# Layer 0's first graph convolution by seven block products, and the first LSTM weights loaded and summed at other places

## The chip, the cores and the metric

The kernel runs on one core of a Trainium2 chip. The metric is the device time of one launch in microseconds (us). Engines: TensorE (PE, with weight loads as PEld), VectorE (DVE), ScalarE (ACT), GpSimd (POOL) and SyncE (SP), which here only issues DMA transfers. All data are float32.

## What is computed

Four layers of a graph network over x, 128 graphs of 64 nodes with 256 features (8192 rows), each added to its input after a layer norm and a ReLU. The change is in layer 0:

```
h = relu(layernorm(x))
h = relu(adj @ (h @ Wg0 + bg0))
h = relu(adj @ (h @ Wg1 + bg1))
for p in 1..4:                      # windows of p nodes
    last = LSTM_p(windows of h)     # Wih[p-1], Whh[p-1], bih + bhh
    h at the last node of each window = last
x = x + h
```

Layers 1 to 3 (edge attention, two products with batch norms, dense attention) follow and stay as they are.

## The kernel before

The stage in question (L453 to L575) makes both graph convolutions for 16 chunks of 512 rows (CHUNK; two graphs fill 128 partitions, so a chunk is four tiles of 128 x 256). For each chunk a generator, graph_convolutions (L502), has five parts, with a yield between them:

1. Norm(...).all() (L78): on VectorE bn_stats and bn_aggr for each of four tiles (L87, L88), a root on ScalarE (L95), reciprocal and shift on VectorE (L96, L97), four scaled ReLUs on ScalarE into h (L109); then x of a later chunk is requested (load_x, L466).
2. aggregate (L139): eight products of 128 columns on TensorE with bdA, the block-diagonal adjacency, and two copies on VectorE into aggT (L145), whose halves k are features and whose columns are the chunk's nodes.
3. The first convolution: for each of two output halves c, two products of 512 columns with quarters of wg0 add up in a bank; VectorE adds bg0 times the row sums of adj (rsum) into h1T (L516), ScalarE takes the ReLU (L524). All products go through the helper mm, so L50 is the line of every one of them, and their tiles tell them apart: aggT,wg is this one.
4. The second convolution: eight products of 256 columns (wg,h1T), VectorE adds bg1 (L539), the result reuses aggT.
5. The second aggregation: eight products of 128 columns (bdA,aggT), ReLUs on ScalarE into hT or hop (L555); chunks 8 to 15 go to memory (hm).

The main loop over n starts chunk n and advances each chunk under way by one part: the newest first, then from the oldest on. So in turn n TensorE makes the second aggregation of chunk n - 4, the second convolution of n - 3, the first of n - 2 and the aggregation of n - 1. From n = 3 on, each step also advances a generator of tables for layers 1 and 2 (edge_tables, late_tables): mostly VectorE operations of 128 x 512, among them four DMA fills of a scatter field (L319), 2.3 MB each, on SP.

The order of an engine's queue is fixed before the launch by the framework's planner: from the program order as priority, it issues what it estimates to be ready first. An instruction passed to late() may not go ahead of what stands before it on its engine in program order. [...]

After turn 2 three sets of LSTM weights are made (Weights, L424): each is one 1 MB transfer on SP (L429) and four sums or differences of quarters on GpSimd, 128 x 512 each (L440). They are the operands of the LSTM's own products, which already use seven products of quarters (L651), with copies on ScalarE (L694, L699) and sums on VectorE (L695, L705, L710). The LSTM starts after the stage. A similar helper, quarter_sums (L126), makes layer 2's operands (L136). Eight PSUM banks are shared by the whole stage; a bank is free again when its last reader is done.

## Time and profile before

| what | value |
|---|---|
| time, median of 3 runs | 2069.58 us (2069.1 to 2072.04) |
| profiled execution: its own time | 2061.03 us |
| profiled execution: span of the core | 2059.3 us |
| TensorE busy in the span | 2006.1 us |
| first product of the LSTM starts at | 192.77 us |
| GpSimd busy in the span | 308.2 us |
| first convolution, 128 products' records of 128 x 512 | 58.5 us as recorded |

Recorded lengths of products overlap, so the pace of TensorE is read from start to start. A product of float32 shows as two records. In the rows, "out<-in" names tiles; behind it stand the shapes, the count, and busy time with the mean in ns, or in a timeline the start and length in us and in brackets the idle time before with what ended it. In the table of busy times each engine has the busy us of the stretch and a count of instructions.

### The profile page before, as it was taken

To read this page: it belongs to the slowest core of one execution; us is meant where nothing else is said; L and a number is where in the kernel's file an instruction comes from. 1 tells how busy PE (TensorE), PEld (TensorE's weight loads), DVE (VectorE), ACT (ScalarE), POOL (GpSimd) and SP (SyncE) were. 2 spreads that over 40 slices of the span, in tenths; PEclk is the share of its full clock that TensorE was granted. 3 is DMA by queue.
4 is the path that set the end of the run, shared out by engine and by line. 5 is a ranking of instruction groups with operands and counts; after the bars stand their busy time and mean duration, and the time that the engine had idled before them with its cause. 6 is when DMAs were issued, how large, how long until landed. Compare 5 with 4: busy or idle time off the path is not lost. (4 is left out here: it accounts for less than half of the span.)

```text
span 2059.3 us, 25491 instructions
## 1 busy us (share of the span) xinstructions
PE 2006.1 (97%) x9444; PEld 1346.1 (65%) x9444; DVE 1359.5 (66%) x2507; ACT 1184.4 (58%) x2230; POOL 308.2 (15%) x416
## 2 busy tenths in 40 slices
PE   8999999999999999999999999999999999999998
PEld 6777478866688845887667887333334775444786
DVE  8755666564565477566556555677777877886776
ACT  4344766555565457566446564666675556591544
POOL 3000010020110020002001000323223420000563
PEclk9999999999999999999999999999999999999999
DMA  9331000100100170001001003412223841022012
GB/s 316 98 98 51 0 21 1 42 0 1 41 1 1 40 246 21 1 0 42 0 1 41 1 16 120 138 61 97 72 98 122 298 154 52 0 82 82 32 62 72
DMA packets 63196, 135.06 MB, mean 66 GB/s; under 512 B 6240, under 2 KB 40928, under 8 KB 60768
## 3 DMA queue, kind: packets, MB, share of 16 engines
q1 hardware_dynamic: 56832, 109.11, 15.6%
q0 software_dynamic: 5632, 24.12, 3.1%
q8 instruction: 74, 1.21, 0.2%
q14 instruction: 50, 0.41, 0.1%
q10 hardware_dynamic: 608, 0.20, 0.0%
HBM read 87.28 MB, written 46.14 MB: 65 GB/s over the span
## 5 line engine op out<-in xcount | busy, mean ns | idle before, releaser
L651 PE MATMUL pa<-xop,sih 128*128 128x256 f32 (+2 forms) x1056 | 344.4, 418 | 11.7 <-DVE gate L705 8.2
L679 ACT ACTIVATE gate<-gate,bias 128x256 f32<-128x256 f32 (+2 forms) x368 | 247.4, 679 | 173.6 <-DVE gate L695 91.0
L651 PEld LDWEIGHTS pa<-xop,sih 128*128 128x128 f32 x1056 | 198.4, 190 | 87.9 <-issue 22.8
L651 PE MATMUL pc<-xop,wih 128*128 128x256 f32 (+2 forms) x736 | 251.2, 423 | 0.0
L695 DVE TENSOR_TENSOR gate<-pb,gate 128x256 f32<-128x256 f32 (+2 forms) x184 | 87.5, 475 | 225.7 <-PE pb L651 154.1
L651 PE MATMUL pa<-lstm_h,shh 128*128 128x256 f32 (+1 forms) x672 | 212.7, 398 | 0.0
L993 DVE SCALAR_TENSOR_TENSOR lr<-lr 128x1024 f32<-128x1024 f32 x128 | 151.1, 1222 | 55.3 <-ACT lr L992 55.3
L651 PEld LDWEIGHTS pc<-xop,wih 128*128 128x128 f32 x736 | 139.8, 190 | 51.2 <-issue 23.0
L710 DVE TENSOR_TENSOR gate<-pc,gate 128x256 f32<-128x256 f32 (+2 forms) x184 | 87.6, 476 | 121.2 <-PE pc L651 120.9
L992 ACT COPY lr<-pair 128x1024 f32<-128x1024 f32 x128 | 123.1, 1014 | 47.6 <-PE pair L986 47.6
L651 PEld LDWEIGHTS pa<-lstm_h,shh 128*128 128x128 f32 x672 | 127.7, 190 | 30.2
L651 PE MATMUL pc<-lstm_h,whh 128*128 128x256 f32 (+1 forms) x448 | 141.8, 398 | 0.0
L694 ACT COPY gate<-pa 128x256 f32<-128x256 f32 (+2 forms) x184 | 76.1, 413 | 96.7 <-PE pa L651 96.1
L986 PE MATMUL pair<-sd_hot,xq 64*128 64x512 f32 x512 | 127.5, 616 | 0.3 <-ACT lr L992 0.3
L705 DVE TENSOR_TENSOR gate<-pa,gate 128x256 f32<-128x256 f32 (+2 forms) x184 | 87.5, 475 | 44.0 <-PE pa L651 43.4
L970 PE MATMUL bank<-wlv,hT 128*128 128x512 f32 x240 | 110.7, 604 | 0.0
L699 ACT COPY gate<-pa 128x256 f32<-128x256 f32 (+2 forms) x184 | 75.4, 410 | 59.1 <-PE pa L651 57.9
L679 ACT ACTIVATE gate<-pa,bias 128x256 f32<-128x256 f32 (+2 forms) x184 | 94.0, 511 | 23.6 <-PE pa L651 22.0
L440 POOL TENSOR_TENSOR sih<-wih 128x512 f32<-128x512 f32 x8 | 10.7, 1335 | 630.6 <-DMA wih<-in_WihT 484.4
L651 PE MATMUL pa<-xop,wih 128*128 128x256 f32 (+1 forms) x320 | 101.4, 398 | 2.7 <-ACT xop L632 2.7
L651 PE MATMUL pb<-xop,wih 128*128 128x256 f32 (+1 forms) x320 | 100.3, 398 | 0.4 <-DVE gate L695 0.4
L651 PEld LDWEIGHTS pc<-lstm_h,whh 128*128 128x128 f32 x448 | 85.1, 190 | 20.1
(346 smaller groups left out, 3809.2 us busy)
## 6 DMA issues: line engine op xcount, KB each, us to landing
field<-sd_hot SPq DMA_DIRECT2D x4, 2304.0 KB, 17.2
wih<-in_WihT SPq DMA_DIRECT2D x8, 1024.0 KB, 5.1
xres<-in_x SPq DMA_DIRECT2D x16, 512.0 KB, 4.6
xa<-xres POOLq DMA_DIRECT2D x16, 512.0 KB, 5.2
dense<-field POOLq DMA_DIRECT2D x4, 2048.0 KB, 8.5
xin<-xb SPq DMA_DIRECT2D x16, 512.0 KB, 3.4
h<-xb SPq DMA_DIRECT2D x16, 512.0 KB, 3.2
xin<-in_x SPq DMA_DIRECT2D x15, 512.0 KB, 3.9
```

Source lines behind the costliest of these rows:

```text
L440: nc.gpsimd.tensor_tensor(o, x, y, op)
L651: ins = nc.tensor.matmul(p[:, : self.N], weights[kind, self.phase](k, q), x[k], start=first_ and kind == "ih", stop=kind == "hh" or not se ...
L679: nc.scalar.activation(out, in_, AF.Tanh if q == 2 else AF.Sigmoid, bias=bias[:, self.w - 1, 2 * q + j : 2 * q + j + 1],)
L694: nc.scalar.copy(blk[0, 0], pa[:, :N])
L695: nc.vector.tensor_tensor(blk[0, 0], pb[:, :N], blk[0, 0], ALU.add)
L699: nc.scalar.copy(blk[1, 0], pa[:, :N])
L705: nc.vector.tensor_tensor(blk[1, 1], pa[:, :N], blk[1, 1], ALU.add)
L710: nc.vector.tensor_tensor(blk[1, 0], pc[:, :N], blk[1, 0], ALU.add)
L970: ins = nc.tensor.matmul(p, hTs[n][:, k, i * P : (i + 1) * P], wlv[:, k, :], start=k == 0, stop=k == 1)
L986: ins = nc.tensor.matmul(p[:, par, :], queries[it][r, c * P : (c + 1) * P], sd_hot[r, :], start=True, stop=True)
L992: nc.scalar.copy(lr, p)
L993: nc.vector.scalar_tensor_tensor(lr, lr, 0.2, lr, ALU.mult, ALU.max)
```

## The change

The first convolution's 256 x 256 matrix is cut into four 128 x 128 quarters, and a chunk's aggT into four blocks of 128 features x 256 nodes. Seven products of one (sum of) quarters with one (sum of) blocks take the place of the eight quarter products (four of 512 columns). The sums of quarters are made once. Per chunk GpSimd forms four differences of blocks (side), and adds the bias rb (rsum times bg0) to three of the four output blocks; ScalarE copies three products out of PSUM, VectorE adds the rest in four sums of 256 columns, the last with the fourth bias. Three products accumulate in bank pa on what stands there, one in pc.

The generator now has twelve parts (four for the norm, one for the aggregation and the differences, four for the products, one for the second convolution, two for the second aggregation), and a written order says which chunk's next part comes when within a turn. x is requested with the aggregation, a turn later. The tables advance at five places of a turn. The three sets of LSTM weights are requested after turns 5, 7 and 9; their sums are issued two per turn from turn 6 on, each behind late().

```diff
--- before.py
+++ after.py
@@ -422,7 +422,7 @@
 
 
         class Weights:
-            def __init__(self, kind, w):
+            def __init__(self, kind, w, at_once=True):
                 bufs = 2 if kind == "ih" else 1
                 t = wsp.tile([P, 2, 4, 2, P], F32, tag=f"w{kind}", name=f"w{kind}", bufs=bufs)
                 s = wsp.tile([P, 3, 4, P], F32, tag=f"s{kind}", name=f"s{kind}", bufs=bufs)
@@ -431,14 +431,22 @@
                 )
                 a11, a12, a21, a22 = t[:, 0, :, 0, :], t[:, 1, :, 0, :], t[:, 0, :, 1, :], t[:, 1, :, 1, :]
                 s1, s2, s4 = s[:, 0], s[:, 1], s[:, 2]
-                for o, x, y, op in (
+                self.sums = [
                     (s1, a21, a22, ALU.add),
                     (s2, s1, a11, ALU.subtract),
                     (s4, a12, s2, ALU.subtract),
                     (a21, a11, a21, ALU.subtract),
-                ):
-                    nc.gpsimd.tensor_tensor(o, x, y, op)
+                ]
+                self.at_once = at_once
+                while at_once and self.sums:
+                    self.sum()
                 self.of = {1: a11, 2: a12, 3: s4, 4: a22, 5: s1, 6: s2, 7: a21}
+
+            def sum(self):
+                o, x, y, op = self.sums.pop(0)
+                ins = nc.gpsimd.tensor_tensor(o, x, y, op)
+                if not self.at_once:
+                    late(ins)
 
             def __call__(self, k, q):
                 return self.of[k][:, q, :]
@@ -460,6 +468,7 @@
 
             xin = cpool("xin", 4)
             g0 = cpool("g0", 5)
+            g0s = cpool("g0s", 2)
             wc = cpool("wc", 1)
             hop = cpool("hop", 3)
 
@@ -497,30 +506,86 @@
             p = bank()
             mm(p[:, :T], ones[:T, :], adjT2[:T, :])
             nc.vector.tensor_copy(rsum, p[:, :T])
-            rsum_b = rsum.unsqueeze(1).to_broadcast([P, 8, T])
+
+            rb = wc.tile([P, 2, T], F32, tag="rb", name="rb")
+            s_g0 = wc.tile([P, 3, 1, P], F32, tag="s_g0", name="s_g0")
+            left = quarter_sums(wg0.rearrange("p k (q j m) -> p k q j m", q=1, j=2), s_g0)
+
+            for c in range(2):
+                nc.gpsimd.tensor_scalar(rb[:, c, :], rsum, bg0[:, c : c + 1], None, ALU.mult)
+
+            def nodes4(ap):
+                return ap.rearrange("p (b t) -> p b t", t=T)
 
             def graph_convolutions(n):
 
-                h = Norm(coming.pop(n), True).all()
+                norm = Norm(coming.pop(n), True)
+                for step in range(2):
+                    for i in range(2):
+                        norm.stats(2 * step + i)
+                    if step:
+                        norm.roots()
+                    yield
+                for step in range(2):
+                    for i in range(2):
+                        norm.scaled(2 * step + i)
+                    yield
                 if 4 <= n + 3 < NCH:
                     coming[n + 3] = load_x(n + 3)
-                yield
+                h = norm.h
                 aggT = g0.tile([P, 2, CHUNK], F32, tag="aggT", name="aggT")
                 h1T = g0.tile([P, 2, CHUNK], F32, tag="h1T", name="h1T")
                 aggregate(h, bdA, aggT)
-                yield
-                for c in range(2):
-                    p = bank()
-                    for k in range(2):
-                        mm(p, wg0[:, k, c * P : (c + 1) * P], aggT[:, k, :], k == 0, k == 1)
-                    nc.vector.scalar_tensor_tensor(
-                        h1T[:, c, :].rearrange("p (b t) -> p b t", t=T),
-                        rsum_b,
-                        bg0[:, c : c + 1],
-                        p.rearrange("p (b t) -> p b t", t=T),
-                        ALU.mult,
-                        ALU.add,
+
+                side = g0s.tile([P, 4, 256], F32, tag="side", name="side")
+                b11, b21, b12, b22 = (
+                    aggT[:, k, u * 256 : (u + 1) * 256] for u in range(2) for k in range(2)
+                )
+                for o, x, y in (
+                    (0, b12, b11),
+                    (2, b22, side[:, 0]),
+                    (1, b22, b12),
+                    (3, b21, side[:, 2]),
+                ):
+                    nc.gpsimd.tensor_tensor(side[:, o], x, y, ALU.subtract)
+                right = {1: b11, 2: b21, 3: b22, 4: side[:, 3], 5: side[:, 0], 6: side[:, 2], 7: side[:, 1]}
+                yield
+
+                def product(k, p, first_=False):
+                    nc.tensor.matmul(
+                        p, left[k][:, 0, :], right[k], start=first_, stop=True, skip_group_check=True
                     )
+
+                def biased(c, blk):
+                    nc.gpsimd.tensor_tensor(
+                        nodes4(blk), nodes4(blk), rb[:, c].unsqueeze(1).to_broadcast([P, 4, T]), ALU.add
+                    )
+
+                pa, pb, pc = (bank()[:, :256] for _ in range(3))
+                blk = {(c, u): h1T[:, c, u * 256 : (u + 1) * 256] for c in range(2) for u in range(2)}
+                product(1, pa, True)
+                product(2, pb, True)
+                nc.scalar.copy(blk[0, 0], pa)
+                nc.vector.tensor_tensor(blk[0, 0], pb, blk[0, 0], ALU.add)
+                biased(0, blk[0, 0])
+                yield
+                product(6, pa)
+                nc.scalar.copy(blk[1, 0], pa)
+                biased(1, blk[1, 0])
+                product(7, pc, True)
+                nc.scalar.copy(blk[1, 1], pc)
+                biased(1, blk[1, 1])
+                yield
+                product(5, pa)
+                nc.vector.tensor_tensor(blk[1, 1], pa, blk[1, 1], ALU.add)
+                yield
+                product(4, pc)
+                nc.vector.tensor_tensor(blk[1, 0], pc, blk[1, 0], ALU.add)
+                product(3, pa)
+                nc.vector.tensor_tensor(
+                    nodes4(blk[0, 1]), nodes4(pa), rb[:, 0].unsqueeze(1).to_broadcast([P, 4, T]), ALU.add
+                )
+                for c in range(1, -1, -1):
                     nc.scalar.activation(h1T[:, c, :], h1T[:, c, :], AF.Relu)
                 yield
                 z = aggT.rearrange("p c t -> p (c t)").rearrange("p (i d) -> p i d", i=4)
@@ -553,24 +618,37 @@
                     for i in range(4):
                         mm(p[:, i * P : (i + 1) * P], z[:, i, c * P : (c + 1) * P], bdA)
                     nc.scalar.activation(dst[:, c, :], p, AF.Relu)
+                    if c:
+                        break
+                    yield
                 if n >= NCH // 2:
                     nc.sync.dma_start(out=hmem[n], in_=dst)
+                yield
 
             tables = chain(edge_tables(), late_tables())
-            under_way = []
+            chunks = {}
+
+
+            order = (2, 0, 4, 0, 2, 4, 1, 0, 2, 3, 0, 2)
             for n in range(NCH + 4):
                 if n < NCH:
-                    under_way.append(graph_convolutions(n))
-
-                for one in under_way[-1:] + under_way[:-1] if n < NCH else list(under_way):
-                    if next(one, 0) == 0:
-                        under_way.remove(one)
-                    if n >= 3:
+                    chunks[n] = graph_convolutions(n)
+                for at, back in enumerate((0, 0, 0, 0) + tuple(b for b in order if b) if n < 4 else order):
+                    if n - back in chunks:
+                        next(chunks[n - back])
+                    if n >= 3 and back and at % 2 == 0:
                         next(tables, None)
+
+                    if n >= 6 and at % 5 == 4:
+                        for w_ in weights.values():
+                            if w_.sums:
+                                w_.sum()
+                                break
                 if n == 2:
-                    weights["ih", 0], weights["ih", 1] = Weights("ih", 1), Weights("ih", 2)
-                    weights["hh", 1] = Weights("hh", 2)
                     nc.vector.tensor_tensor(bias, bias, bias2, ALU.add)
+                if n in (5, 7, 9):
+                    kind, ph = {5: ("ih", 0), 7: ("ih", 1), 9: ("hh", 1)}[n]
+                    weights[kind, ph] = Weights(kind, ph + 1, False)
             for _ in tables:
                 pass
 
```

## The prediction

> **What bounds the kernel now.** I read the page first, then the order of TensorE's (PE's) work in layer 0, its waits there, and busy time turn by turn.
>
> ```profile
> PE 2006.1 (97%) x9444; PEld 1346.1 (65%) x9444; DVE 1359.5 (66%) x2507; ACT 1184.4 (58%) x2230; POOL 308.2 (15%) x416
> ```
> TensorE is the bound: 97% busy, GpSimd (POOL) 15%. What leaves TensorE's queue ahead of the LSTM should therefore shorten the span, if nothing new waits.
>
> The timeline of TensorE alone, one turn in mid-stage and the stage's end (start, length, line, operands):
>
> ```profile
> 80.66 3.62 PE L50 MATMUL bank<-wg,h1T 128*128 128x256 f32 x16
> 84.12 3.60 PE L50 MATMUL bank<-aggT,wg 128*128 128x512 f32 x8
> 87.55 1.95 PE L50 MATMUL bank<-bdA,h 128*128 128x128 f32 x16
> 89.33 1.95 PE L50 MATMUL bank<-bdA,aggT 128*128 128x128 f32 x16
> 91.12 3.62 PE L50 MATMUL bank<-wg,h1T 128*128 128x256 f32 x16
> ...
> 190.82 2.11 PE L50 MATMUL bank<-bdA,aggT 128*128 128x128 f32 x16
> 192.77 1.02 PE L651 MATMUL pa<-hT,wih 128*128 128x512 f32 x2
> ```
> From start to start, the first convolution (L50 aggT,wg) holds TensorE 87.55 - 84.12 = 3.43 us: four products of 512 columns (two records each), 0.86 us apiece. The second (wg,h1T) takes 84.12 - 80.66 = 3.46 us for eight products of 256 columns: 0.432 each. A turn is 10.46 us, with no gap, and the LSTM's first product follows at once. TensorE's waits in the first 200 us:
>
> ```profile
> PE bank L50 <- ACT h L109: 3.9, 1, 3.9
> PE bank L50 <- DVE bdH L222: 3.2, 1, 3.2
> PE bank L50 <- ACT h1T L524: 1.5, 1, 1.5
> PE bank L50 <- DVE aggT L145: 1.4, 2, 1.2
> ```
> All belong to the start (the latest, on h1T, is at 42 us). VectorE's (DVE's) margin is smaller; these columns are PE, PEld, DVE, ACT, POOL, PEclk, DMA share, GB/s:
>
> ```profile
> 33.06:45.26 12.20, 10.73 (x58) 8.05 (x57) 12.10 (x38) 5.90 (x13) 0.38 (x1) 1.00 1.08 379
> 84.12:94.58 10.46, 10.46 (x58) 8.13 (x57) 10.39 (x25) 4.63 (x9) 0.00 (x0) 1.00 0.16 50
> 171.69:182.15 10.46, 10.46 (x57) 8.13 (x56) 4.26 (x6) 2.45 (x4) 0.00 (x0) 1.00 0.13 52
> ```
> The edge tables fill VectorE up to 100 us or so; after them it idles half the time.
>
> **TensorE.** The change removes four products of 512 columns and adds seven of 256, at the second convolution's pace: 3.43 - 7 x 0.432 = 0.40 us per chunk, 6.4 us over 16. The weight loads stay covered: 14 x 190 ns = 2.66 us beside 3.03. Aggregations and the second convolution are the same work, only split.
>
> **VectorE and ScalarE.** The nearest rows are the LSTM's seven products, at 256 columns, in the first 400 us:
>
> ```profile
> L695 DVE TENSOR_TENSOR gate<-pb,gate 128x256 f32<-128x256 f32 x28 | 11.8, 421 | 27.0 <-PE pb L651 19.0 <-ACT gate L694 5.1 <-PE pa L651 2.9
> L694 ACT COPY gate<-pa 128x256 f32<-128x256 f32 x28 | 10.3, 369 | 11.2 <-PE pa L651 10.9
> ```
> VectorE loses two 743 ns bias steps (L516) and gains four sums of 421: +0.20 us per chunk. ScalarE (ACT) gains three copies of 369: +1.11, on some 4 to 6 us in a turn of 10, which is cover enough.
>
> **GpSimd.** Seven two-input operations of 128x256 per chunk. Line 136 has them in another layer:
>
> ```profile
> L136 POOL TENSOR_TENSOR w1S<-w1T x1: 723/723/723, 1300.4 to 1300.4; 128x256 f32<-128x256 f32 x1
> L136 POOL TENSOR_TENSOR w1T<-w1T x1: 1787/1787/1787, 1301.9 to 1301.9; 128x256 f32<-128x256 f32 x1
> ```
> 0.72 us undisturbed, so 5.0 us per turn; 1.79 at worst, so 12.5, which would outrun a turn. Six of the eight rows of L136 have 0.72 to 0.74, so I take 0.72. Two weight sums (L440, 1.27) in each of six turns make it 7.6 of 10.05. A rule speaks against this placing: the Trainium skill (GPSIMD Engine Reference, 4.1 Engine selection) sends two-input elementwise work to VectorE, as GpSimd takes about twice as long. The rows say 0.72 against 0.42, 1.7 times. But by the rule the seven would put 7 x 0.42 = 2.9 us on a VectorE with 10.39 of 10.46 us taken: some 3 us more per turn there. On GpSimd they fit, unless the two engines hold each other up. They do, in the VectorE timeline; GpSimd runs the weight sums from 17.64 to 33.44 us:
>
> ```profile
> 8.90 0.41 DVE L304 CAST iota<-wide 128x512 f32<-128x512 int32 x1
> 26.23 0.75 DVE L516 SCALAR_TENSOR_TENSOR h1T<-rsum,bg,bank 128x512 f32<-128x512 f32 x1 [0.97 <-PE bank L50]
> 29.28 1.36 DVE L306 CAST wide<-wide 128x512 f32<-128x512 int32 x1
> 30.67 1.64 DVE L309 SCALAR_TENSOR_TENSOR wide<-wide,iota 128x512 f32<-128x512 f32 x1
> ```
> The same cast goes from 0.41 to 1.36 us; L309 takes 1.64 where the like L349 takes 0.69; L311 takes 1.23 where a small cast takes 0.16, L97 0.55 instead of 0.15. In all 3.4 us lost beside 15.8 us of GpSimd: 0.21 us per us. L516, reading PSUM, keeps its 0.75. The skill (SBUF — State Buffer, Who interferes with whom) states the rule: a VectorE instruction with two SBUF inputs, or in a two-port mode, shares a locked port with GpSimd, and the later one is blocked for the whole instruction; with one SBUF input it is not. So the new VectorE sums (PSUM plus SBUF) are safe, while the tables and L97 are exposed, some five operations a turn. By the rule at its worst each waits a whole 0.72: 3.6 us a turn. By the rows: 0.21 x 5.0 = 1.1 us, or 1.6 beside weight sums. I take the rows.
>
> What this costs TensorE: in the seven turns from 33.06 to 105.04 us VectorE is busy 60.3 of 72.0 us (the stretches added up). They gain 7 x 0.20 of sums and, five of them beside weight sums, 5 x 1.6 + 2 x 1.1 of lock waits: 71.9, where seven shortened turns leave 72.0 - 2.8 = 69.2. That is 2.7 us over; but h and aggT are used a turn after VectorE makes them ready, so its queue may lag some us unnoticed, and afterwards it has time to catch up. Bounds: 0 and 3 us; I charge 1.0.
>
> **The chain inside a chunk.** P6 waits for ScalarE's copy of P1's bank, P5 for the next copy, P3 for VectorE's sum, behind other queue entries; behind each waiting product stands all of TensorE's queue. Aggregations (0.89 each half) and the second convolution (3.46) stand between them and cover copies of 0.37 and sums of 0.42. The LSTM has the same chain, and from 200 to 300 us TensorE is busy 99.14 of 100. In steady turns I charge nothing; at most 1.3 us by that row over 150 us. Two banks are held nearly a whole turn out of eight; no row prices it, and it lies within that bound. At the start GpSimd's four differences (2.9 us in series) follow the first aggregation with little work beside them. But TensorE already idles 2.3 us between 11.65 and 17.36 there, and chunk 1's aggregation can slip in. Bounds: -2.5 us (the waits of 1.2 and 1.5 us vanish) to +2; I charge 0.4. The one-time sums of wg0 (four, 128 wide, below 0.72 each) and two small rb products run before the first aggregation ends.
>
> **What moves.** Three 1 MB transfers leave SP's queue at 9.7, 13.7 and 14.3 us and go behind the x loads, the small table loads and the four field fills, which hold SP from 26.7 to 45.6 us with DMA share near 1 until about 60. The x loads move one turn later, still over a turn ahead of use. Twelve weight sums go behind block sums and differences on GpSimd. A sum that waits for a late transfer holds up the next biases and differences, and so P6 and P5. Sums begin about 52 us, and some 18 MB in all pass by 60, so a wait of a few us is possible once; I count it in the 0 to 3 us above. The LSTM reads these weights from 192 us; the last sum falls near 110.
>
> **The sum.** -6.4 + 1.0 + 0.4 = -5.0 us. The profiled execution took 2061.03 us (span 2059.3, 1.7 around it); it becomes 2056.0. The timed median lies 8.5 us above that profile; I carry this over unchanged: 2069.58 - 5.0 = 2064.6.
>
> **Rivals.** *Start improves too* (0.20): the early weight sums no longer hold up VectorE, so the 1.47 us wait at 42 us goes, and up to 1 us beside the bias load. 6.4 + 2.5 = 8.9 us: 2060.7. For it: those slowed rows. Against: the differences now press on the same tables. *Chain exposed* (0.17): 0.25 us of waits per turn, about one late copy, gives back 4 us: 2067.2. For it: P6 and P5 wait behind ScalarE's in-order queue, with a root that waits on VectorE. Against: 99.14 of 100 above. *VectorE held by GpSimd becomes the bound* (0.13, slower): at twice the measured rate, 0.42 us per us, and with no lag allowed, one of the seven table turns needs 60.3 / 72.0 x 10.46 = 8.8, + 0.2 + 3.2 = 12.2 us beside weight sums (five, +1.74 over 10.46) and 11.1 without (two, +0.64); the nine others save 0.40 each: 8.7 + 1.3 - 3.6 = +6.4, so 2076.0. It decides from +0.5 us in each table turn, which is 2.0 us of lock waits. For it: the 3.6 us of the rule at its worst. Against: GpSimd's operations are half as long as the sums that gave 0.21. *Weights not later at all*: their loads wait for nothing, so the planner may put them early again; worth nothing at 192 us.
>
> **Numbers.** Forecast case 0.50 (2062.5 to 2066.5), rivals as given. About 0.2%, 4.1 us, is what a measurement of this kernel can tell from no change. Faster: 0.40 of the forecast case plus 0.20 = 0.60; same: 0.10 + 0.17 = 0.27; slower: 0.13. The range 2060.5 to 2071 leaves out the slower rival and some of the first.
>
> **What would show it.** Right: the LSTM's first product near 188 us, a steady turn of 10.05, seven 256-column products at 0.43, GpSimd near 0.72 per operation. Wrong: TensorE waits on the new sums or the differences between 45 and 110 us, VectorE table rows stretched past 1 us, GpSimd waiting for wih.

## The result, and the profile after

The changed kernel took 2075.53 us (median of 8 runs, 2073.86 to 2079.15) beside 2068.95 us (8 runs, 2067.91 to 2072.79) for the kernel before: a ratio of 1.0031, interval 1.0020 to 1.0041. It is 6.6 us slower, where the forecast was 5 us faster; 2075.53 lies outside the stated range, and within half a microsecond of the rival *VectorE held by GpSimd becomes the bound* (2076.0).

The profiled execution of after took 2075.05 us, span 2072.9. The two profiles' spans are not compared here: some 8 us of their difference arose in layer 1, far behind the change (last section). What is compared is the start of the LSTM's first product, called *the mark* below, which was at 192.77 us before, and the timed medians. The page's first row after:

```profile
PE 2011.9 (97%) x9540; PEld 1372.5 (66%) x9540; DVE 1366.1 (66%) x2539; ACT 1200.8 (58%) x2278; POOL 389.8 (19%) x534
```

GpSimd's 118 new instructions are there, and TensorE is busy longer, not shorter (in part for the stretch in layer 1 just named). TensorE's waits up to the mark:

```profile
PE bank L50 <- ACT h L109: 3.9, 1, 3.9
PE bank L50 <- DVE bdH L222: 3.0, 1, 3.0
PE bank L50 <- DVE aggT L604: 3.0, 3, 1.3
PE bank L555 <- DVE aggT L145: 2.8, 1, 2.8
PE bank L555 <- ACT h1T L568: 2.6, 3, 1.2
```

The first two stood before as well, and the fourth belongs to the start (13.98 us). The third and fifth are new and belong to mid-stage: VectorE's sums of z, the second convolution's output plus its bias (L604, written into the tile named aggT), and ScalarE's copy of a product's bank (L568). The timeline of TensorE shows where they are; first a turn beside the edge tables, then a quiet one, then the mark:

```profile
74.78 3.62 PE L50 MATMUL bank<-wg,h1T 128*128 128x256 f32 x16
78.23 0.59 PE L555 MATMUL bank<-side,wg 128*128 128x256 f32 x2
...
79.96 0.61 PE L50 MATMUL bank<-bdA,aggT 128*128 128x128 f32 x4
81.67 0.71 PE L50 MATMUL bank<-bdA,aggT 128*128 128x128 f32 x4 [1.10 <-DVE aggT L604]
...
83.50 0.70 PE L555 MATMUL bank<-side,s_g 128*128 128x256 f32 x2 [0.69 <-ACT h1T L568]
...
170.69 1.05 PE L50 MATMUL bank<-bdA,aggT 128*128 128x128 f32 x8
171.83 0.67 PE L555 MATMUL bank<-side,s_g 128*128 128x256 f32 x2
...
195.97 1.02 PE L729 MATMUL pa<-hT,wih 128*128 128x512 f32 x2
```

Four of the seven products take the 1.73 us from 78.23 to 79.96, 0.43 each, as predicted. But the second aggregation (bdA,aggT) now starts 79.96 - 78.23 = 1.7 us behind the second convolution whose sums it reads. Before, the first convolution and an aggregation lay between them: 89.33 - 84.12 = 5.2 us. The mark came at 195.97, 3.2 us late. Busy time in a turn beside the tables and in a quiet one (us, then PE, PEld, DVE, ACT, POOL, PEclk, DMA share, GB/s):

```profile
74.78:87.15 12.37, 10.58 (x64) 9.27 (x63) 12.30 (x29) 3.44 (x9) 7.46 (x10) 1.00 0.14 43
165.51:175.88 10.37, 10.28 (x63) 9.35 (x62) 4.18 (x9) 5.16 (x11) 4.96 (x8) 1.00 0.13 51
```

In the long turn VectorE has 12.30 of 12.37 us taken and runs late. (Being full is not enough: before it had 10.39 of 10.46, and TensorE waited for nothing.) What fills it, in its timeline:

```profile
77.05 0.86 DVE L361 TENSOR_SCALAR same<-wide,pair 128x512 f32<-128x512 f32 x1
...
78.88 0.67 DVE L604 TENSOR_TENSOR aggT<-bank,bg 128x512 f32<-128x512 f32 x1
79.86 1.09 DVE L364 SCALAR_TENSOR_TENSOR same<-iota,index,same 128x512 f32<-128x512 f32 x1
...
80.97 0.65 DVE L604 TENSOR_TENSOR aggT<-bank,bg 128x512 f32<-128x512 f32 x1
```

Before, L361 took 0.45 to 0.49 and L364 0.73 to 0.75, for instance:

```profile
79.65 0.47 DVE L361 TENSOR_SCALAR same<-wide,pair 128x512 f32<-128x512 f32 x1
81.42 0.73 DVE L364 SCALAR_TENSOR_TENSOR same<-iota,index,same 128x512 f32<-128x512 f32 x1
```

In after's turn they took 0.86 and 1.09. The second L604, for which TensorE waits, stands behind L364. Sums that read PSUM keep their length (0.65 to 0.67).

**Where 3.2 us come from.** TensorE's busy time to the mark was 182.78 of 192.77 us before, so 9.99 us idle: 8.52 up to the first second-convolution product at 19.14, and 1.47 later. Take off the 6.4 us saved, and 176.4 of work are left; the mark at 195.97 then means 19.6 us of waits: 9.8 up to 24.41 (24.41 less 14.62 busy) and 9.8 behind it. So -6.4 of work, +1.3 at the fill, +8.3 in the stage: +3.2. (Busy time after, 180.19, includes waits too short to show as gaps.) The split is good to about 1 us, because part of the busy time ahead of the fill is products at half the granted clock (0.50 from 14.1 to 17.5 us). Measured against e15 below, whose stage of 162.5 us has the same products and one wait of 0.2, after's stage lost 171.6 - 162.3 = 9.2 us, 7.7 more than before's, and the fill's share is 1.9. Of the stage's 9.8, four turns of 12.33, 12.37, 11.65 and 11.68 us, beside 10.05 without waits, make 7.8; the quiet turns of 10.3 to 10.37 make most of the rest.

### The profile page after: what moved, and what is told of

It is laid out like the page before. It is cut to its first block, busy times and chain, and to the rows that moved or that the text cites. A ratio compares the mean times of both kernels' runs of the same rounds, so it can differ in the third digit from the quotient of the medians.

```text
span 2072.9 us, 25968 instructions
## 1 busy us (share of the span) xinstructions
PE 2011.9 (97%) x9540; PEld 1372.5 (66%) x9540; DVE 1366.1 (66%) x2539; ACT 1200.8 (58%) x2278; POOL 389.8 (19%) x534
## 5 line engine op out<-in xcount | busy, mean ns | idle before, releaser
L447 POOL TENSOR_TENSOR sih<-wih 128x512 f32<-128x512 f32 x8 | 11.0, 1374 | 565.2 <-DMA wih<-in_WihT 419.8
```

## The experiments

The theories, as the expectations use them. *A*: the order alone, because the second aggregation stands too close behind the second convolution. *A2*: VectorE is simply too full beside the tables. *B*: the late weight sums are to blame. *L*: GpSimd's instructions hold VectorE up, by the rule of the shared port that the prediction cites. The *fill* is the start of the first second-convolution product; the *stage* runs from there to the mark. All kernels from after down have the same products in the stage, to within one (0.43 us) in e4, e6 and e16, so their stages can be compared; not so e10, which has plain products in ten chunks, and before, e2 and e14: before's stage has 10.4 us more of TensorE work (182.78 - 10.62 = 172.2, after 176.4 - 14.6 = 161.8). e5, e9, e11 and e12 leave part of the arithmetic out, so their times only serve the comparison.

| kernel | fill | stage | mark | median, before beside it (us) | ratio (interval) |
|---|---|---|---|---|---|
| before | 19.1 | 173.6 | 192.77 | | |
| after | 24.4 | 171.6 | 195.97 | 2075.53, 2068.95 | 1.0031 (1.0020-1.0041) |
| e1 weights early | 26.1 | 175.9 | 202.03 | 2080.87, 2070.56 | 1.0056 (1.0037-1.0076) |
| e2 before, weights late | 19.8 | 172.6 | 192.45 | 2071.01, 2070.56 | 1.0003 (0.9994-1.0012) |
| e3 ReLUs later | 25.0 | 170.1 | 195.10 | 2072.62, 2070.56 | 1.0010 (1.0001-1.0019) |
| e4 aggregation later | 27.3 | 170.9 | 198.21 | 2077.47, 2070.56 | 1.0030 (1.0020-1.0040) |
| e5 no GpSimd per chunk | 25.5 | 164.4 | 189.94 | 2067.98, 2069.82 | 0.9989 (0.9983-0.9996) |
| e6 iotas first | 25.8 | 172.0 | 197.79 | 2077.43, 2069.82 | 1.0036 (1.0024-1.0048) |
| e7 fewer table steps | 25.0 | 173.2 | 198.15 | 2075.79, 2069.82 | 1.0028 (1.0017-1.0040) |
| e8 e3 and e6 | 27.6 | 171.6 | 199.22 | 2075.91, 2069.82 | 1.0027 (1.0015-1.0038) |
| e9 lock only | 25.2 | 173.7 | 198.99 | 2075.26, 2069.55 | 1.0025 (1.0016-1.0034) |
| e10 plain, then seven | 26.1 | 164.1 | 190.25 | 2069.72, 2069.55 | 0.9997 (0.9989-1.0005) |
| e11 no biases on GpSimd | 25.4 | 169.2 | 194.52 | 2070.25, 2069.55 | 1.0004 (0.9994-1.0013) |
| e12 memsets | 25.6 | 163.7 | 189.31 | 2064.84, 2069.55 | 0.9975 (0.9964-0.9987) |
| e13 after again | 27.3 | 172.2 | 199.46 | 2067.78, 2063.01 | 1.0021 (1.0009-1.0034) |
| e14 before again | 20.8 | 172.1 | 192.86 | 2062.34, 2063.01 | 0.9999 (0.9992-1.0006) |
| e15 no GpSimd reads | 26.1 | 162.5 | 188.56 | 2057.44, 2063.01 | 0.9975 (0.9965-0.9986) |
| e16 e15 and e4 | 26.5 | 165.9 | 192.44 | 2063.45, 2063.01 | 1.0004 (0.9995-1.0012) |

Fill, stage and mark are of one profiled execution each. e13 repeats after: its stage agrees within 0.6 us, its fill is 2.9 us later. e14 repeats before: stage within 1.5, fill 1.6 later. By these two repeats a mark is good to some 3 us, a stage to 1 or 1.5.

### e1 to e4: the weights, the ReLUs, the order

e1 is after with the three weights of before's time:

```diff
                 if n == 2:
+                    weights["ih", 0], weights["ih", 1] = Weights("ih", 1), Weights("ih", 2)
+                    weights["hh", 1] = Weights("hh", 2)
                     nc.vector.tensor_tensor(bias, bias, bias2, ALU.add)
-                if n in (5, 7, 9):
...
-                    weights[kind, ph] = Weights(kind, ph + 1, False)
```

> The changed kernel with the three sets of LSTM weights back after turn 2, loaded and summed at once. The mark is the start of the LSTM's first product (192.77 us before, 195.97 after). Theory A (the written order leaves the second aggregation only 1.7 us behind the second convolution, and ScalarE's copy of the first product behind two ReLUs): the waits in the later turns stay, mark 194 to 197. Theory B (the two late weight sums per turn hold up VectorE): the waits on the second convolution's sums between 80 and 105 us shrink, mark near 192, and the start gets 1 to 3 us worse by the sums' return.

Mark 202.03, ratio 1.0056. TensorE's longest wait in it, VectorE's (from another answer of the same view), and what GpSimd did meanwhile:

```profile
PE bank L555 <- DVE h1T L580: 5.1, 1, 5.1
...
DVE h1T L580 <- POOL h1T L560: 7.1, 1, 7.1
```

```profile
28.77 1.27 POOL L447 TENSOR_TENSOR sih<-wih 128x512 f32<-128x512 f32 x1
...
33.77 1.40 POOL L560 TENSOR_TENSOR h1T<-h1T,rb 128x256 f32<-128x256 f32 x2
```

GpSimd took its queue in order: a bias sum stands behind four weight sums (28.77 to 33.8), VectorE behind the bias, TensorE behind VectorE. The first two turns of the stage took 30.7 us, where after has 22.6. Theory B is right in a part, though: with no weight sums beside the tables the four turns that took 12.37, 10.28, 11.65 and 11.68 us in after take 11.07, 10.05, 10.54 and 10.70 (3.6 us less). As the whole of the loss it falls: spreading the sums gains 4.4 us of stage on balance (175.9 less 171.6).

e2 is before with the weights alone late and spread (after's `Weights` class, and a `sum()` at two places of a turn):

> The kernel before, with only the weights moved: loads after turns 5, 7 and 9, sums two per turn from turn 6. Theory A: TensorE has 5.2 us between the second convolution and the second aggregation in this order, so late sums cost nothing, and the 1.5 us wait at 42 us of the kernel before goes: mark 191 to 192.5. Theory B: waits appear between 50 and 110 us, mark 194 to 196.

Mark 192.45, ratio 1.0003: alone the move is worth nothing that can be measured. 

e3 issues the two h1T ReLUs one part later, behind the copies that they stood ahead of on ScalarE:

```diff
-                for c in range(1, -1, -1):
-                    nc.scalar.activation(h1T[:, c, :], h1T[:, c, :], AF.Relu)
+                relus[n] = [h1T[:, c, :] for c in range(1, -1, -1)]
                 yield
...
                     if n - back in chunks:
                         next(chunks[n - back])
+                    if back == 4:
+                        for r_ in relus.pop(n - 3, ()):
+                            nc.scalar.activation(r_, r_, AF.Relu)
```

> The changed kernel with the two ReLUs on h1T issued a part later, in the next turn behind the first half of the second aggregation, so that ScalarE copies the next chunk's first product before them. Theory A: the quiet turns (140 to 185 us) fall from 10.37 to 10.05 us, and of the waits in the table turns those on ScalarE's copy (2.6 us) go and those on the second convolution's sums (3.0 us) stay: mark 191 to 193. Theory B: the mark stays within 1 us of 195.97.

The quiet turns became 10.05, so this chain is what cost them 0.3 us. In after's timeline of ScalarE, the copy that the product at 171.83 waits for stands behind the ReLUs, and these waited for VectorE's sum L583:

```profile
170.28 1.15 ACT L589 ACTIVATE h1T<-h1T 128x512 f32<-128x512 f32 x2 [2.96 <-DVE h1T L583]
171.34 0.35 ACT L568 COPY h1T<-bank 128x256 f32<-128x256 f32 x1
```

Beside the tables the waits stayed (2.8 us on z's sums, 2.0 on copies, 1.2 on L580): stage -1.4, ratio 1.0010.

e4 moves the second aggregation two parts back:

```diff
-            order = (2, 0, 4, 0, 2, 4, 1, 0, 2, 3, 0, 2)
+            order = (2, 0, 1, 0, 2, 4, 2, 0, 4, 3, 0, 2)
```

> The changed kernel with one change in the written order: the aggregation of chunk n - 1 goes ahead of the sixth and seventh products, and the halves of the second aggregation behind them. The second aggregation then starts 4.4 us behind the second convolution instead of 1.7, and 1.8 us instead of 0.9 cover ScalarE's copy. Theory A: the waits on the second convolution's sums and on the copy go, a quiet turn takes 10.05 us, mark 187 to 191, the time 5 to 9 us below that of the changed kernel. Theory B: the waits stay, mark within 1.5 us of 195.97.

The wait on z's sums went, quiet turns fell to 10.05, and turns of 12.30 and 13.08 stayed: in the stage TensorE now waited for the copies (3.3 us), for h (1.1) and for VectorE's sums L580 (0.9). Stage 170.9, ratio 1.0030. With VectorE late, another order only changes which product waits. Theory A, the order alone, falls.

### e5 to e8: GpSimd's work, the fill, fullness

e5 leaves the seven GpSimd operations of each chunk out; its products take undifferenced quarters and no bias comes on:

```diff
...
-                    nc.gpsimd.tensor_tensor(side[:, o], x, y, ALU.subtract)
-                right = {1: b11, 2: b21, 3: b22, 4: side[:, 3], 5: side[:, 0], 6: side[:, 2], 7: side[:, 1]}
+                    pass
+                right = {1: b11, 2: b21, 3: b22, 4: b21, 5: b12, 6: b22, 7: b12}
...
-                    nc.gpsimd.tensor_tensor(
-                        nodes4(blk), nodes4(blk), rb[:, c].unsqueeze(1).to_broadcast([P, 4, T]), ALU.add
-                    )
```

> The changed kernel without the seven GpSimd operations of a chunk: the four differences of blocks and the three biases are left out, the products take plain blocks instead, so part of layer 0's arithmetic is missing; TensorE, VectorE and ScalarE have the same instructions, and the weights' sums stay. Theory A1 (GpSimd's port lock and its serial differences make VectorE late in the table turns): the table turns fall to 10.1 to 10.5 us and the mark to 187 to 190. Theory A2 (VectorE is simply too full there for an order that leaves the second aggregation 1.7 us): the table turns stay above 11 us, mark 193 to 196; the quiet turns stay at 10.37 in both, since ScalarE's queue is untouched.

Stage 164.4, 7.2 us less than after: most of the 9.2 us that the stage lost hang on GpSimd's seven operations, by waiting for their results or by theory L. The mark is in A1's range; the quiet turns take 10.25, where 10.37 was expected.

e6 sets up node_i and index_i (two iotas) ahead of wg0's sums, since VectorE waited 1.90 us for them at the fill; e8 is e3 and e6 together:

> The changed kernel with the tables' two small iotas (L290, L292) issued on GpSimd ahead of the sums of wg0 and the bias products, instead of behind them. Theory: VectorE's 1.9 us wait on node_i at 9.7 us, which holds up chunk 1's statistics and aggT's copies, is a queue effect of the new wg0 sums; the first second-convolution product then starts near 22.5 us instead of 24.4, mark 193.5 to 194.5. If aggT's copies wait for something else (the bias transfer that lands at 13.8 us), the mark stays within 0.5 us of 195.97.

> The changed kernel with both repairs: ReLUs a part later (e3) and iotas first (e6). If the two add: mark 195.97 - 0.9 - 1.9, near 193.2, quiet turns 10.05, and a time within 2 us of the kernel before; if they hide the same wait, mark near 195.

Both missed. Their stages (172.0, 171.6) are after's within the spread; the fill did not shrink (25.8, 27.6). VectorE's wait on node_i went, but it then waited 1.7 us (e8: 2.1) for another iota (L287), so these runs do not test the fill without such a wait; and e13's fill is 27.3 with no edit.

e7 takes the tables at three places of a turn, where after has five:

```diff
-                    if n >= 3 and back and at % 2 == 0:
+                    if n >= 3 and back and at % 2 == 0 and (at > 2 or n < 4):
```

> The changed kernel with the tables advanced at three places of a turn instead of five, from turn 4 on, so that VectorE's table work is spread up to the last turns. Theory A2 (VectorE full): the long turns (12.4, 11.7, 11.7 us) fall below 10.8, mark 190 to 193. Theory A1 (the lock alone): the same number of table operations meets GpSimd as before, so the waits are spread rather than gone, mark 194 to 196.

Stage 173.2: no gain from spreading the same work over more turns, against A2. The mark, 198.15, lies above A1's range too; stronger evidence against A2 is in e12.

### e9 to e12: which property of GpSimd's work it is

e9 keeps seven two-input GpSimd operations at the same places, but they read only aggT and rb and write to a tile that nobody reads; the products take plain blocks, the bias goes nowhere. In its stage no engine waits for GpSimd any more:

```diff
...
-                right = {1: b11, 2: b21, 3: b22, 4: side[:, 3], 5: side[:, 0], 6: side[:, 2], 7: side[:, 1]}
+                right = {1: b11, 2: b21, 3: b22, 4: b21, 5: b12, 6: b22, 7: b12}
...
-                        nodes4(blk), nodes4(blk), rb[:, c].unsqueeze(1).to_broadcast([P, 4, T]), ALU.add
+                        nodes4(side[:, c]), nodes4(right[1 + c]), rb[:, c].unsqueeze(1).to_broadcast([P, 4, T]), ALU.add
```

> The changed kernel with the same seven GpSimd operations per chunk, each reading two tiles in SBUF, but writing to a tile that nobody reads; the products take plain blocks, so differences and biases are left out of the result. GpSimd still competes for the port; nothing waits for it. Theory L (the port lock makes VectorE late): mark 194 to 197, table turns still above 11 us, VectorE's table rows still stretched. Theory C (TensorE, VectorE and ScalarE wait for GpSimd's results in series): mark 189 to 191.5, as without the operations (189.9).

It is as slow as after (stage 173.7, ratio 1.0025), and TensorE's waits on z's sums are still there:

```profile
PE bank L50 <- DVE aggT L604: 3.7, 4, 1.7
```

So no wait for GpSimd's results is needed for the loss; that it runs and reads beside VectorE is enough.

e12 issues 14 GpSimd memsets of 128x256 per chunk instead of the seven operations, so that GpSimd writes but, apart from the weights' sums, reads nothing; four products take the zeroed tile:

```diff
-                    nc.gpsimd.tensor_tensor(side[:, o], x, y, ALU.subtract)
...
+                for o in range(14):
+                    nc.gpsimd.memset(side[:, o % 4], 0.0)
```

> The changed kernel with fourteen GpSimd memsets of 128x256 per chunk in place of the seven operations that read (differences and biases are left out of the result, the products take the zeroed tile): GpSimd is busy for about as long, but reads nothing from SBUF. Theory L in the form that a VectorE instruction with two SBUF inputs is held only by a GpSimd instruction that reads: mark 189 to 191.5 and table rows at their plain lengths. If any GpSimd work holds VectorE up: mark 193 to 197.

Stage 163.7, ratio 0.9975: faster than before, though it computes less. GpSimd was not idle in it: it was busy for 81.47 us to the mark, 59.8 more than in e5, where e9 has 80.7 more. A turn beside the tables, as after's long one above:

```profile
73.89:83.94 10.05, 10.05 (x64) 9.28 (x63) 9.98 (x27) 3.77 (x10) 5.86 (x16) 1.00 0.18 53
```

VectorE is as full (9.98 of 10.05 us), and TensorE waits for nothing: fullness alone, A2, is not the cause. GpSimd's timeline and VectorE's in one stretch:

```profile
88.05 3.89 POOL L545 MEMSET side<- 128x256 f32 x14 [3.11 <-PE bank L550]
91.92 1.26 POOL L447 TENSOR_TENSOR wih<-wih 128x512 f32<-128x512 f32 x1
93.15 1.72 POOL L447 TENSOR_TENSOR shh<-whh 128x512 f32<-128x512 f32 x1
```

```profile
90.47 0.47 DVE L361 TENSOR_SCALAR same<-wide,pair 128x512 f32<-128x512 f32 x1
...
92.18 1.55 DVE L364 SCALAR_TENSOR_TENSOR same<-iota,index,same 128x512 f32<-128x512 f32 x1
```

L361, in the middle of the memsets, has its plain 0.47; L364, beside two weight sums (which read), takes 1.55 where 0.73 is plain. VectorE's 382 instructions up to the mark took 130.90 us here, 131.77 in e5, 140.58 in e9 and 139.75 in after: the reads of GpSimd stretch VectorE by some 9 us, and the stage by 7.8 (after) to 10.0 (e9). That GpSimd's reads delay VectorE and so TensorE is shown; the port itself no trace shows.

e11 leaves only the three biases out: stage 169.2, 2.4 us less than after, where e5 without all seven has 7.2 less. Three sevenths of the operations give a third of the loss.

> The changed kernel without the three GpSimd biases of a chunk (left out of the result); the four differences stay and the products use them. Theory L: the lock's cost falls with GpSimd's reads, three sevenths of some 6 us: mark 193 to 194.5. Theory C with the differences on the path: mark 195 to 196; with the biases on the path: 190 to 191.

e10 keeps the four plain products for chunks 0 to 9, beside the tables, takes the seven for chunks 10 to 15, and has e4's order:

> A version made for speed: chunks 0 to 9 with the plain four products, chunks 10 to 15 with the seven, in the order of e4 (second aggregation later) and with the weights late. Where the tables fill VectorE, GpSimd then has only the weights' sums; where VectorE is half idle, a turn takes 10.05 instead of 10.46 us. Mark 192.5 - 6 x 0.4 = 190 to 191, time 1.5 to 2.5 us below the kernel before. If the seven products lose in the quiet turns too, mark 192.5 or more.

Mark 190.25, table turns of 10.46, quiet ones of 10.05: the saving is real where VectorE has nothing else to do. In the timed runs 0.9997 (0.9989 to 1.0005) doesn't show the 1.5 to 2.5 us that were expected.

### e13 to e16: repeats, and a version without GpSimd

e13 and e14 are after and before once more, in the runs of e15 and e16:

> The changed kernel once more, for the spread of the mark between executions. If the first profile is typical, the mark is 195 to 197; if VectorE and GpSimd meet differently from run to run, it may lie 2 us or more higher, which would explain that the timed difference (6.6 us) is larger than the mark's (3.2).

> The kernel before once more. Mark 192.3 to 193.3. Layer 1's stretch of 112 us to its last output product, in which the first profile of the kernel before is some 7.5 us shorter than every other profile so far, should come out like the others, and the span near 2067 us; if it comes out short again, the shorter stretch belongs to the kernel before and is part of the difference.

After was slower again (1.0021), before equal to itself (0.9999).

e15 keeps the seven products and takes GpSimd out of the chunk. ScalarE copies the aggregate out of PSUM, VectorE forms the differences with one operand still in PSUM, and the bias goes onto the ReLU instead of a sum (three ReLUs a chunk, where after has two): the first aggregation is divided by the row sums of the adjacency (bd1) and the second multiplied by them (bd2), with bg1 divided to fit. The ReLUs come a part later, as in e3:

```diff
-                aggregate(h, bdA, aggT)
+                for c in range(2):
+                    p = bank()
...
+                        mm(p[:, i * P : (i + 1) * P], h[:, i, c * P : (c + 1) * P], bd1)
+                    nc.scalar.copy(aggT[:, c, :], p)
...
-                    nc.gpsimd.tensor_tensor(side[:, o], x, y, ALU.subtract)
+                for o, x, y in ((0, q12, b11), (2, q22, side[:, 0]), (1, q22, b12), (3, q21, side[:, 2])):
+                    nc.vector.tensor_tensor(side[:, o], x, y, ALU.subtract)
...
+                        for r_, b_ in relus.pop(n - 3, ()):
+                            nc.scalar.activation(r_, r_, AF.Relu, bias=b_)
```

> A version that keeps the seven products but leaves GpSimd no operation per chunk: ScalarE copies aggT out of PSUM, VectorE forms the differences from PSUM (one SBUF input each), and the bias rides on ScalarE's ReLUs, with the first adjacency divided by its row sums and the second multiplied by them; ReLUs a part later as in e3. Theory L (reads of GpSimd hold VectorE): VectorE's load per turn is about that of the kernel before (6.9 us without tables) and nothing holds it, so table turns at 10.05 to 10.5, mark 188.5 to 190.5, time 3 to 5 us below the kernel before. If VectorE's fullness is the cause, table turns stay above 11 us and the mark above 193.

2057.44 us beside 2063.01: ratio 0.9975 (0.9965 to 0.9986), the only version of the whole computation here that beats both kernels. As it also moves the ReLUs and the copies of the aggregate, it is no test of one cause; that is e9 and e12. Its stage in busy time (columns as above), and TensorE's only listed wait in it:

```profile
26.05:188.56 162.51, 162.34 (x958) 144.09 (x957) 113.04 (x326) 100.61 (x217) 16.54 (x13) 1.00 0.38 130
```

```profile
PE bank L50 <- DVE aggT L603: 0.2, 1, 0.2
```

TensorE is busy 162.34 of 162.51 us, and its mark, 188.56, is that of the forecast (near 188).

e16 is e15 with e4's order:

> The same with the order of e4 (aggregation of n - 1 ahead of the sixth product, second aggregation behind the seventh). Theory L: the order no longer matters once VectorE is in time, mark within 1 us of e15. If the 1.7 us behind the second convolution still bind, mark 1 to 2 us lower than e15.

A miss: one turn took 17.39 us where e15's has 14.35, stage 165.9, ratio 1.0004. TensorE waited once for 3.2 us on ScalarE's copy of a product bank (its L577). In e4's order TensorE has 1.3 us of other work between the sixth product and the fifth, which needs this copy; in after's it has 3.1.

## Why the prediction was wrong

**TensorE's saving: right.** 0.43 us per product, 10.05 us per turn in e3, e4, e10 and e15, 6.4 us in all. In e15 4.2 of them reach the mark (192.77 to 188.56): its stage waits 0.17 us where before's waited 1.47, its fill 26.05 - 14.49 = 11.6 us where before's waited 8.5.

**Lengths of the new operations: right.** GpSimd 0.72 to 0.74 mostly, VectorE's sums 0.41 (421 ns foretold), ScalarE's copies 0.35 to 0.37 (369 ns). VectorE's sums from PSUM kept their length beside GpSimd.

**"I charge 1.0" for the lock: the step that failed.** The lock waits themselves were sized about right: the prediction put 5 x 1.6 + 2 x 1.1 = 10.2 us onto VectorE beside the tables, and after minus e12 has 139.75 - 130.90 = 8.9 us up to the mark (without what the weights' sums cost alone, since e12 has them too). What failed was the next sentence, that VectorE's "queue may lag some us unnoticed", since "h and aggT are used a turn after". That holds for the copies of h and the aggregate. It doesn't hold for z's sums, which the list of consumers left out: the new order leaves them 1.7 us where before's left 5.2, and a two-input table operation of 0.73 us that becomes 1.09 stands ahead of one. Nor does it hold for the sum L583, on which the ReLUs and so the copies hang. Measured as stages, the price is 171.6 - 163.7 = 7.8 us (e13: 8.4), not 0 to 3: nearly all that VectorE lost reached TensorE. e12 also drops the waits for GpSimd's results, so this is the price of both; e9, with the reads alone, has all of it (173.7).

**"In steady turns I charge nothing": wrong by 0.3 us a turn.** The copy of P1's bank stands behind two ReLUs of 1.15 us together that wait for VectorE, and little more than half an aggregation (0.89 us) is all that TensorE has to do meanwhile; e3 takes the wait away. The LSTM's row was no measure of this slack: there a copy (L699 at 205.91) stands behind an activation of 1.15 us that waited for VectorE, too, and TensorE was still busy for 99.14 of 100 us. This was the rival *chain exposed* (0.25 us per turn), and it came true beside the other one.

**The fill: +0.4 charged; +1.3 in the first pair of profiles, +1.9 in the second**, both within its bounds of -2.5 to +2 (idle time up to the fill: after 9.8 and before 8.5, e13 11.1 and e14 9.1). The 2.3 us taken for idle in before were 1.4 of gaps (0.21 and 1.22); the rest was products at a slower pace, eight records of 512 columns in 4.45 us where later 3.60 is usual. Of *start improves too*, only the 1.5 us wait at 42 us went. The spread between executions of the same kernel, 2.9 us, is larger than what was argued about, and the granted clock makes part of it. In e13 the first product (aggT,wg) started 1.6 us later than in after, 1.0 of it a longer wait for aggT. The 54 records from there to the fill then took 1.3 us longer (after, then e13; the clock is the third column from the end):

```profile
13.98:24.41 10.43, 10.43 (x54) 8.76 (x54) 8.83 (x34) 6.31 (x15) 8.39 (x12) 0.84 0.80 266
15.58:27.29 11.71, 11.71 (x54) 10.07 (x55) 8.83 (x34) 6.29 (x15) 8.43 (x12) 0.74 0.77 260
```

10.43 x 0.84 is 8.8 and 11.71 x 0.74 is 8.7, so the clock accounts for these 1.3 us.

**The weights: "worth nothing at 192 us" was right for before (e2), and wrong in place.** Within the new convolution their move is worth 4.4 us of stage (e1): 8.0 gained in the first two turns, because GpSimd's queue now has something that others wait for behind those sums, and 3.6 lost beside the tables.

**The slower rival was right that VectorE's lateness reaches TensorE, and lucky in its size.** At its rate of 0.42, GpSimd would have cost VectorE 5 x 3.2 + 2 x 2.1 = 20.2 us; the runs have 8.9, near the forecast's own 10.2. What came true is its other half, "no lag allowed". Its turns of 12.2 us beside weight sums and 11.1 without are not those that came: four turns took 12.3, 12.4, 11.65 and 11.7, the first of them with no weight sum beside it, and the other turns did not save the whole 0.40 us, as the ReLUs took most of it. So its total, +6.4, met the timed +6.6 by luck: the two profiles of after have the mark at +3.2 and +6.7, the fill deciding. e11 and e5 show that the loss goes about with the number of operations.

**Still open.** Why spreading the tables (e7) gained nothing; why the first wait for aggT and the granted clock differ between executions of one kernel; and whether e10's gain is there in time.

## What to carry to other kernels

Price a GpSimd operation that reads SBUF twice: by its own length (0.73 us here, hidden), and by what it adds to the VectorE operations beside it (8.9 us for 112 of them here). Then follow every result of VectorE that stands behind those to its consumer, by name, in the new order. An order that is rewritten to fit new work gives each other chain a new slack (here 1.7 us for 5.2), so list old and new slack for all of them before charging nothing. Where a short elementwise operation can take one operand from PSUM, or ride on an activation as its bias, it need not be on GpSimd: in e15 such a difference took VectorE 0.42 us, and L361 and L364 kept their plain lengths (0.47 to 0.49 and 0.73 to 0.75).

## What the runs showed of the hardware

**What GpSimd did to the VectorE instruction beside it depended on whether it read.** L364, with two SBUF inputs, went from 0.73 to 1.55 us beside two-input sums (e12, above). L385, a comparison of two SBUF tensors, took 1.42 us beside such sums in e9, and in the middle of e12's memsets 0.68, as in before (0.66 and 0.68); here e9, then e12:

```profile
62.96 1.45 POOL L447 TENSOR_TENSOR sih<-sih,wih 128x512 f32<-128x512 f32 x1
63.54 1.42 DVE L385 TENSOR_TENSOR first<-wide 128x511 f32<-128x511 f32 x1
...
64.08 4.15 POOL L545 MEMSET side<- 128x256 f32 x14 [6.20 <-PE bank L550]
65.32 0.68 DVE L385 TENSOR_TENSOR final<-wide 128x511 f32<-128x511 f32 x1
```

Both agree with the rule in the Trainium skill (SBUF — State Buffer, Who interferes with whom) by which a VectorE instruction with two SBUF inputs contends with a GpSimd instruction that reads, not with one that only writes. Instructions with one SBUF tensor as input were stretched, too: L361 took 0.86 beside reads. Memsets left L361 alone (0.47 to 0.49), but not all of its kind: L331 took 0.53 to 0.60 in the middle of memsets where 0.45 to 0.49 is plain, and L306 0.61 where 0.43 is. The section's bullet on two-port modes would allow that; the trace doesn't tell in which mode an instruction ran. In one case at least the one that came second was held: in after L364 started at 96.51 and kept its 0.73 us, and GpSimd's L447, which started at 96.57, took 1.79 where 1.27 is plain.

**A stretch of layer 1 takes 112 or 119 us, whatever the kernel.** From the first to the last product with wout before's profile took 1668.5 - 1556.6 = 111.9 us, and e13 to e16, after and before among them, 111.9 to 112.0. After's first profile took 1681.2 - 1560.7 = 120.5, e1 to e12 119.2 to 119.4, e2 with before's convolution too. In the slow form TensorE stops four times for 0.3 to 0.4 us with nothing to wait for that the profile shows (in after from 1585.94 us, in e2 from 1581.76); that is 1.6 of the 7.4 us, and the rest lies in the same first 80 us of the stretch. In after the granted clock, the third column from the end, then fell by half:

```profile
1584.00:1588.00 4.00, 2.51 (x63) 1.56 (x60) 1.60 (x2) 0.00 (x0) 3.09 (x3) 0.95 0.10 29
1588.00:1592.00 4.00, 3.58 (x13) 3.01 (x13) 0.00 (x0) 0.00 (x0) 3.08 (x4) 0.50 0.08 25
```

In e2 it stayed at 1.00 there and the loss was nearly the same (119.3), so the clock explains about 1 us of it; the cause of the rest is open. In the runs of e13 to e16 both kernels were some 7 us faster (before 2063.01, after 2067.78), with their difference nearly as it was. That fits the 8.5 us by which before's profile lay under its median, which the prediction carried over unexplained, and it is why only times taken together are compared here.
